# Five projections of a two-layer graph attention kernel: from a 7-product scheme on halves to a 15-product scheme on thirds

## The chip, the cores and the metric

The kernel runs on one core of a Trainium2 chip. The metric is the device time of one execution in microseconds; the time before is the median of three runs, 644.64 us (644.09 to 644.74). All data is fp32 apart from masks. The engines named below are TensorE (PE: matmuls; PEld: its weight loads), VectorE (DVE), ScalarE (ACT), GpSimd (POOL) and SyncE (SP), and the 16 DMA engines that carry out the transfers that SP, POOL and ACT issue.

## The reference

A graph attention network of two layers on 512 nodes with 768 features, a residual and a layer norm. Layer 1 has 8 heads, layer 2 has one.

```python
def gat_layer(x, W, a_s, a_d, b, edge_index, concat):
    n = x.shape[0]
    H, C = a_s.shape
    h = (x @ W).reshape(n, H, C)
    src, dst = (edge_index[0], edge_index[1])
    alpha_s = jnp.einsum('nhc,hc->nh', h, a_s)
    alpha_d = jnp.einsum('nhc,hc->nh', h, a_d)
    e = jax.nn.leaky_relu(alpha_s[src] + alpha_d[dst], NEG_SLOPE)
    m = jax.ops.segment_max(e, dst, num_segments=n)
    e = jnp.exp(e - m[dst])
    denom = jax.ops.segment_sum(e, dst, num_segments=n)
    alpha = e / (denom[dst] + EPS)
    msg = h[src] * alpha[:, :, None]
    out = jax.ops.segment_sum(msg, dst, num_segments=n)
    out = out.reshape(n, H * C) if concat else out.mean(axis=1)
    return out + b

h = gat_layer(x, W1, a_src1, a_dst1, b1, edge_list, concat=True)   # W1 768 x 6144
h = jax.nn.elu(h)
out = gat_layer(h, W2, a_src2, a_dst2, b2, edge_list, concat=True) # W2 6144 x 768
x = _layernorm(x + out, axis=-1)
```

The projection is `x @ W`: for one head 512 x 768 by 768 x 768.

## The kernel before

The edges are counted once into a dense 512 x 512 matrix (`cnt`), so that attention is a masked softmax times this count, and the sums over edges are matmuls. The heads of layer 1 then go through a loop (L874 to L977), and each pass of it has three stretches of work on TensorE:

- `mixed` (L783): the attention matrix of head h+1 times its features, 21 products of 256 columns, which gives the transposed output of the head; `elu` (L736) writes it to `gT`.
- `second` (L358): `gT` of that head times its 768 rows of W2, added into `h2`.
- `projection` (L333): x times the columns of W1 of head h+2, into `hs`.

Each of the three uses a scheme of seven products for blocks of 2 x 2 (halves of 256 nodes and of 384 features). For the projection there are 7 products x 2 row tiles of 128 nodes x 3 parts of the sum (`product`, L311), 42 matmuls of 128 x 128 by 128 x 384. The operands on the left, `XA`, are blocks of the transposed x (`xT`) and three sums of such blocks (`xS`); they are made once (`left`, L290), one of them in place in `xT`. The operands on the right are blocks of the weights and four sums: `t1` and `t3` are made while loading, by a plain transfer from SP and an accumulating one from POOL onto it (L107/L108, L119); `t2` and `t4` by VectorE (L307, L308).

The order on each engine's queue is written out by hand: an instruction stands in its engine's queue where the program calls it (`manual_schedule`). What matters around the change:

- Weights have two slots. `load_w1(h + 2)` goes into slot "w2" at the top of a pass (L876). `load_w2(h + 1)` goes into slot "w1" at the end of `second` (L949), behind the four transposing transfers of the attention matrix (`turn_out`, L730). For each, SP issues `t1` and six blocks of 128 rows, POOL the two additions (0.59 MB each).
- `attended` (L859) loads operands into `w2t2` and `w2t4`; VectorE reads them (`attend`) right after the projection's first product has been issued.
- In the projection's loop (L954 to L974) VectorE empties the banks of PSUM (ten of fourteen, L350 to L354; ScalarE the others), makes the sums for the next `mixed` (`left_sums`, `right_sums`), the sums of the weights of the coming `second` (`sums2`), and the logits of two node tiles. The pool `mm` has five banks.
- `row_out` (L474) sends a row of logits through DRAM by SP, to be broadcast; `lift` (L486) of the next `second` reads it.

## Time and profile before

| What | us |
|---|---|
| median of three runs | 644.64 |
| the profiled execution | 644.97 |
| its span, first to last instruction | 643.2 |
| granted clock of TensorE, mean share | 0.999 |
| one pass of the loop (227.05 to 299.61) | 72.56 |
| in it: `mixed`, `second` and projection | 18.38, 54.18 together |
| VectorE busy in that `mixed`, `second`, projection | 14.72, 21.98, 20.66 |

The page gives per group of instructions the source line, the engine, the operation, the output and inputs by the program's names, the shape, the count, the busy time and the mean ns of one instruction. The line is that of the helper, so all products of `projection` and `second` stand under L315, and are told apart by their tiles: `xT` and `xS` are the projection's, `gT` and `gS` those of `second`. An fp32 matmul is two instructions. In a timeline each line has the start, the length, the engine, the source line, the operation and its tiles; SPq and POOLq are the queues that issue transfers. In a table of stretches each line has the stretch, its length, the busy time and the instructions of PE, PEld, DVE, ACT and POOL, the granted clock, the busy share of the DMA engines and what they moved in GB/s.

### The profile page before, as it was taken

To read this page: it belongs to the slowest core of one execution; us is meant where nothing else is said; L and a number is where in the kernel's file an instruction comes from. 1 tells how busy PE (TensorE), PEld (TensorE's weight loads), DVE (VectorE), ACT (ScalarE), POOL (GpSimd) and SP (SyncE) were. 2 spreads that over 40 slices of the span, in tenths; PEclk is the share of its full clock that TensorE was granted. 3 is DMA by queue.
4 is the path that set the end of the run, shared out by engine and by line. 5 is a ranking of instruction groups with operands and counts; after the bars stand their busy time and mean duration, and the time that the engine had idled before them with its cause. 6 is when DMAs were issued, how large, how long until landed. Compare 5 with 4: busy or idle time off the path is not lost.

```text
span 643.2 us, 7161 instructions
## 1 busy us (share of the span) xinstructions
PE 633.0 (98%) x2329; PEld 403.0 (63%) x2329; DVE 515.8 (80%) x1124; ACT 281.9 (44%) x476; POOL 46.2 (7%) x90
## 2 busy tenths in 40 slices
PE   8999999999999999999999999999999999999995
PEld 5555586557755586556755586556855586645553
DVE  8979889978789777877789677877789677876775
ACT  5874745530726045530726045430726035543440
POOL 1300011011000010011000110011000110000000
PEclk9999999999999999999999999999999999999999
DMA  8993488796706794196716794196806890410222
GB/s 295 326 235 88 84 239 276 161 267 202 190 21 170 157 254 139 35 267 193 197 29 162 165 256 139 33 264 202 191 30 155 219 258 16 107 50 0 32 59 77
DMA packets 81096, 100.32 MB, mean 156 GB/s; under 512 B 39654, under 2 KB 63006, under 8 KB 81054
## 3 DMA queue, kind: packets, MB, share of 16 engines
q1 hardware_dynamic: 67646, 78.57, 39.5%
q0 software_dynamic: 12976, 20.65, 18.5%
q10 hardware_dynamic: 432, 0.59, 0.3%
q8 instruction: 20, 0.33, 0.2%
q14 instruction: 22, 0.18, 0.1%
HBM read 86.93 MB, written 1.59 MB: 138 GB/s over the span
## 4 chain that ended last, share of the span: by engine, by line
PE 97%; ACT 1%; DVE 1%; issue 0%; DVEq 0%; ACTq 0%
PE mm L315 65%; PE mm L805 20%; PE mm L751 3%; PE mm L1086 3%; PE held L315 2%; PE tr L580 1%; PE bc L184 1%; PE held L460 1%; PE bc L580 0%; ACT os L552 0%; PE mm L213 0%; PE tr L1010 0%; DVE os L554 0%; PE tr L719 0%; ACT xT L214 0%
## 5 line engine op out<-in xcount | busy, mean ns | idle before, releaser
L315 PE MATMUL mm<-w,gT 128*128 128x384 f32 x288 | 96.3, 487 | 0.0
L315 PE MATMUL mm<-w,xT 128*128 128x384 f32 x264 | 88.2, 487 | 0.0
L315 PEld LDWEIGHTS mm<-w,gT 128*128 128x128 f32 x288 | 54.5, 190 | 37.2 <-issue 1.6
L315 PEld LDWEIGHTS mm<-w,xT 128*128 128x128 f32 x264 | 49.9, 190 | 35.3 <-ACT os L552 0.8
L809 ACT COPY u<-mm 128x256 f32<-128x256 f32 x21 | 7.8, 373 | 140.5 <-PE mm L805 140.5
L499 ACT ACTIVATE q<-q,nmax 128x512 f32<-128x512 f32 x36 | 25.8, 721 | 88.3 <-DVE nmax L497 88.3
L805 PE MATMUL mm<-PT,hs 128*128 128x256 f32 x252 | 61.3, 379 | 0.0
L315 PE MATMUL mm<-w1t,gS 128*128 128x384 f32 x180 | 60.6, 487 | 0.0
L315 PE MATMUL mm<-w2t,xS 128*128 128x384 f32 x168 | 56.6, 487 | 0.0
L805 PEld LDWEIGHTS mm<-PT,hs 128*128 128x128 f32 x252 | 47.8, 190 | 8.4 <-issue 0.4
L315 PEld LDWEIGHTS mm<-w1t,gS 128*128 128x128 f32 x180 | 34.1, 190 | 24.0 <-DVE w1t L307 0.5
L375 DVE TENSOR_TENSOR h<-h,mm 128x384 f32<-128x384 f32 x72 | 39.1, 550 | 12.5 <-PE mm L315 12.0
L315 PEld LDWEIGHTS mm<-w2t,xS 128*128 128x128 f32 x168 | 31.8, 190 | 22.4 <-ACT q L488 0.4
L805 PE MATMUL mm<-pS,gS 128*128 128x256 f32 x168 | 43.2, 380 | 0.0
L733 ACT COPY PT<-zr 128x1024 uint16<-128x1024 uint16 x34 | 39.5, 1161 | 2.6 <-DMA zr<-pS 2.0
L805 PEld LDWEIGHTS mm<-pS,gS 128*128 128x128 f32 x168 | 31.8, 190 | 4.7 <-DVE pS L778 0.4
L728 ACT COPY pS<-q 128x1024 uint16<-128x1024 uint16 x26 | 27.2, 1044 | 16.7 <-DVE q L713 16.7
L315 PE MATMUL mm<-w,gS 128*128 128x384 f32 x96 | 32.6, 486 | 0.0
L315 PE MATMUL mm<-w,xS 128*128 128x384 f32 x96 | 32.5, 487 | 0.0
L315 PE MATMUL mm<-w1t,gT 128*128 128x384 f32 x96 | 32.3, 486 | 0.0
L375 DVE TENSOR_TENSOR u<-u,mm 128x384 f32<-128x384 f32 x28 | 15.4, 553 | 18.8 <-PE mm L315 18.7
L108 POOL DMA_DIRECT2D w1t<-in_L_gnn_W_dram x7 | 8.9, 1267 | 299.0 <-DVE hs L768 171.7
(192 smaller groups left out, 1080.6 us busy)
## 6 DMA issues: line engine op xcount, KB each, us to landing
w<-in_L_gnn_W_dram SPq DMA_DIRECT2D x91, 384.0 KB
w<-in_L_gnn_W_dram POOLq DMA_DIRECT2D x16, 576.0 KB, 8.6
w2t<-in_L_gnn_W_dram SPq DMA_DIRECT2D x10, 576.0 KB
w1t<-in_L_gnn_W_dram SPq DMA_DIRECT2D x9, 576.0 KB
w2t<-in_L_gnn_W_dram POOLq DMA_DIRECT2D x8, 576.0 KB, 8.9
w1t<-in_L_gnn_W_dram POOLq DMA_DIRECT2D x7, 576.0 KB, 8.5
a_s<-in_L_gnn_a_src_dram SPq DMA_DIRECT2D x8, 384.0 KB
a_d<-in_L_gnn_a_dst_dram SPq DMA_DIRECT2D x8, 384.0 KB
```

Source lines behind the costliest of these rows:

```text
L108: nc.gpsimd.dma_start(t1, upper[:, :, R], accum_op=ALU.add)
L184: nc.tensor.matmul(idle, zeros[:, :P], zeros, start=True, stop=True)
L315: nc.tensor.matmul(ps[:, :HALF], A_[p][:, k, i * P:(i + 1) * P], B_[p][:, k, :], start=start and k == 0, stop=k == HK - 1, skip_group_chec ...
L375: nc.vector.tensor_tensor(a, a, ps, op=ALU.subtract if p == "P7" else ALU.add)
L460: nc.tensor.matmul(bank["P1", i][:, :HALF], XA["P1"][:, k, i * P:(i + 1) * P], B_["P1"][:, k, :], start=k == 0, stop=k == HK - 1, skip_gro ...
L499: nc.scalar.activation(q, q, AF.Exp, bias=nmax, scale=-1.0)
L728: nc.scalar.copy(apart.rearrange("p (h n) -> p h n", h=2), q.bitcast(U16).rearrange("p (n h) -> p h n", h=2))
L733: nc.scalar.copy(PT.rearrange("p s n -> p (s n)").bitcast(U16).rearrange("p (s n h) -> p s n h", s=NT, h=2)[:, :, t * P:(t + 1) * P, :], p ...
L751: nc.tensor.matmul(ps[:, :N], HS[h][:, s, c * P:(c + 1) * P], PT[:, s, :], start=(s == 0), stop=(s == NT - 1))
L805: nc.tensor.matmul(bank[p][:, :HN], A_[p][:, k, c * P:(c + 1) * P], B_[p][:, k, :], start=over is None and k == 0, stop=k == 1, skip_group ...
L809: nc.scalar.copy(u, part("P1"))
L1086: nc.tensor.matmul(ps[:, :cols.stop - cols.start], PT[:, s, t * P:(t + 1) * P], h2[:, s, cols], start=(s == 2), stop=(s == 1))
```

## The change

For heads 3 to 7 the projection uses another scheme. x is cut into 2 halves of nodes and 3 thirds of features, the head's weights into 3 x 3 thirds, and 15 products take the place of the 18 of a plain block product. A product is 2 row tiles x 2 parts of the sum, 4 matmuls of 128 x 128 by 128 x 256, so there are 60 of them. The two row tiles lie beside each other in one bank, and each product is emptied by one instruction of 128 x 512. Five chains of products share five banks; within a chain a product is added to what lies in the bank, after the emptying of the one before.

Fifteen left operands come from x. Three are blocks of `xT` as they are (`P2`, `P4`, `P0`), three are sums put in place of blocks of it (`P8`, `P9`, `P13`), and four sums (`P11`, `P10`, `P12`, `P5`) lie in `xS`. Five (`P7`, `P1`, `P6`, `P3`, `P14`) are made in `gT`, which is overwritten in each pass, so they are stored once to DRAM (`xd`, 128 x 2560) and loaded again ahead of each projection (`reload_x`, behind the transposes and ahead of `load_w2`). They are made in the pass of head 2, whose projection keeps the old scheme, and the last ones in the next `mixed` and `second`.

The weights: `load_thirds` issues six row blocks and two plain blocks of 0.26 MB on SP, and four additions of 0.26 MB on POOL; `rest` issues P11's plain block and its addition after the projection has begun, and VectorE makes eight sums of 512 columns in the projection's loop. The slot "w2" is now one tile of six row blocks, not two of three. Of the two sums of W2 one is made in the projection's last step, the other in the next `mixed`.

The diff, with the parts that only unpack tiles left out:

```diff
+    xdram = ctx.enter_context(tc.tile_pool(name="xdram", bufs=1, space=bass.MemoryType.DRAM))
...
-        W[h] = []
-        for r in range(2):
-            w = wpool.tile([P, HK, D], F32, name=f"{slot}{r}")
-            for k in range(r * HK, (r + 1) * HK):
-                nc.sync.dma_start(w[:, k - r * HK, :], m[k * P:(k + 1) * P, :])
-            W[h].append(w)
-        W[h].append(t1)
+        if slot == "w2":
+            rows_ = wpool.tile([P, DC, D], F32, name="w2r")
+            W[h] = [rows_[:, :HK], rows_[:, HK:], t1]
+        else:
+            W[h] = [wpool.tile([P, HK, D], F32, name=f"{slot}{r}") for r in range(2)] + [t1]
+        for k in range(DC):
+            nc.sync.dma_start(W[h][k // HK][:, k % HK, :], m[k * P:(k + 1) * P, :])
...
+    def load_thirds(h):
...
+        rows_, pair_ = wpool.tile([P, DC, D], F32, name="w2r"), flat(1)
+        add = ALU.add
+        for k in range(DC):
+            nc.sync.dma_start(rows_[:, k, :], m[k * P:(k + 1) * P, :])
+            if k == 3:
+                nc.gpsimd.dma_start(third(rows_, 1, 1), part(1, 2), accum_op=add)
+            if k == 5:
+                nc.gpsimd.dma_start(third(rows_, 2, 1), part(0, 1), accum_op=add)
+        for j, (k0, k1, n) in enumerate(((0, 2, 2), (0, 1, 0))):
+            nc.sync.dma_start(square(pair_, j), part(k0, n))
+            nc.gpsimd.dma_start(square(pair_, j), part(k1, n), accum_op=add)
+        raw = {(k, n): third(rows_, k, n) for k in range(3) for n in range(3)}
+        B_ = dict(P8=raw[0, 2], P9=raw[0, 0], P5=raw[0, 1], P13=square(pair_, 0), P12=square(pair_, 1),
+                  P14=raw[2, 1], P4=raw[2, 0], P0=raw[1, 2], P3=raw[2, 2], P7=raw[1, 0], P1=raw[1, 1])
+        def rest():
+            two, four = flat(2), flat(4)
+            B_.update(P6=square(two, 0), P2=square(two, 1), P11=square(four, 0), P10=square(four, 1))
+            nc.sync.dma_start(B_["P11"], part(0, 1))
+            nc.gpsimd.dma_start(B_["P11"], part(1, 1), accum_op=add)
...
+            return dict(P6=op("P6", "P14", "P4", ALU.subtract), P4=op("P4", "P13", "P4", add),
+                        P2=op("P2", "P12", "P13", ALU.subtract), P10=op("P10", "P5", "P1", add),
+                        P0=op("P0", "P12", "P0", add), P1=op("P1", "P6", "P1", add),
+                        P3=op("P3", "P10", "P3", ALU.subtract), P7=op("P7", "P6", "P7", add))
+        return B_, rest
...
+    def by_thirds(h, A_, B_):
...
+                first = chain not in bank
+                if first:
+                    bank[chain] = mm.tile([P, 512], F32, name="mm")
+                for i in range(2):
+                    for k in range(2):
+                        nc.tensor.matmul(bank[chain][:, i * TH:(i + 1) * TH], A_[p][:, k, i * P:(i + 1) * P], B_[p][:, k, :],
+                                         start=first and i == k == 0, stop=k == 1, skip_group_check=True)
+            def empty():
+                ps = bank[chain].rearrange("p (i n) -> p i n", i=2)
+                if how in (1.0, -1.0):
+                    nc.scalar.activation(out(o), ps, AF.Copy, scale=how)
+                else:
+                    nc.vector.tensor_tensor(out(o), out(o), ps, op=how)
...
+            ("P8", "a", (1, 2), 1.0), ("P13", "x", (1, 2), minus), ("P9", "b", (1, 0), 1.0), ("P2", "y", (0, 0), 1.0),
+            ("P4", "x", (1, 0), plus), ("P12", "y", (1, 0), minus), ("P6", "x", (1, 1), 1.0), ("P0", "y", (1, 2), plus),
+            ("P1", "z", (0, 1), -1.0), ("P10", "y", (1, 1), minus), ("P5", "z", (1, 1), plus),
+            ("P14", "x", (0, 1), minus), ("P11", "y", (0, 1), plus), ("P7", "x", (0, 0), minus),
+            ("P3", "y", (0, 2), -1.0))]
...
+    def x_thirds():
...
+        again_ = op(xT[:, :HK, HN:], xT[:, :HK, :HN], xT[:, :HK, HN:], minus)
+        store = lambda: nc.sync.dma_start(stored, gF[:, :RELOAD * 2 * TH])
...
+    def reload_x():
+        nc.sync.dma_start(gF[:, :RELOAD * 2 * TH], stored)
...
         if 0 < h < H - 2:
-            load_w1(h + 2)()
+            B3, rest_of_thirds = load_thirds(h + 2)
...
-        finish = mixed(h, AA, BB, besides + [d_ for _, d_ in halves])
-        besides = []
+        finish = mixed(h, AA, BB, besides + [d_ for _, d_ in halves] + behind)
+        besides, behind = [], []
...
                 turn_out(q[3], 3)
+                if 0 < h:
+                    reload_x()
                 load_w2(h + 1)()
             e1()
-        if h + 2 < H:
+            for f in in_second[:1]:
+                f()
+            del in_second[:1]
+        if 0 < h and h + 2 < H:
+            for f in attend:
+                f()
+            sums = rest_of_thirds()
+            pairs = by_thirds(h + 2, XB, B3)
+            AA, sums3 = left_sums(h + 1)
+            B2, sums2 = right(W2[h + 1], "w1")
+            for n in range(15):
+                pairs[n][0]()
+                for p in {0: ("P6", "P2"), 1: ("P4",), 4: ("P10",), 5: ("P0",), 6: ("P1",), 9: ("P7",),
+                          12: ("P3",)}.get(n, ()):
+                    sums[p]()
+                if n == 5:
+                    BB, rsums_ = right_sums()
+                    sums3 += rsums_
+                if n in (2, 3, 5, 6, 8, 9, 10):
+                    for _ in range(2 if n == 8 else 1):
+                        sums3.pop(0)()
+                if n in (11, 13):
+                    logits(h + 2, HS[h + 2], 2 + (n - 11) // 2)
+                if n == 14:
+                    sums2[0]()
+                    behind = sums2[1:]
+                pairs[n][1]()
+                if n in (1, 2, 4):
+                    turn_in((n + 2) // 2)
+            assert not sums3
+        elif h + 2 < H:
...
-                if n in (9, 10):
+                if n == 0:
+                    XB, early, again_, store, late_ = x_thirds()
+                if n in (2, 4, 6, 8, 9):
+                    early.pop(0)()
+                if n == 9:
+                    store()
+                if n == 9:
+                    again_()
+                if n == 12:
+                    late_.pop(0)()
                     sums2.pop(0)()
+                    behind = sums2 + late_[:2]
+                    in_second = late_[2:]
```

More of the change, by code (lines that the diff above doesn't have):

```diff
@@ L121, in load_w, with third, square, part @@
         return rest
+    TH = 2 * P
+    def third(rows_, k, n):
+        return rows_[:, 2 * k:2 * k + 2, n * TH:(n + 1) * TH]
+    def square(t_, j):
+        return t_[:, j * 2 * TH:(j + 1) * 2 * TH].rearrange("p (k n) -> p k n", k=2)
+    def load_thirds(h):
+        m = w1[:, h * D:(h + 1) * D]
+        def part(k, n):
+            return m[k * TH:(k + 1) * TH, n * TH:(n + 1) * TH].rearrange("(k p) d -> p k d", p=P)
+        def flat(j):
+            return wpool.tile([P, HK, HALF], F32, name=f"w2t{j}").rearrange("p k n -> p (k n)")
+        rows_, pair_ = wpool.tile([P, DC, D], F32, name="w2r"), flat(1)
[17 more added lines that the diff above has]
+            nc.gpsimd.dma_start(B_["P11"], part(1, 1), accum_op=add)
+            def op(o, a, b, how):
+                return lambda: nc.vector.tensor_tensor(B_[o], B_[a], B_[b], op=how)
+            return dict(P6=op("P6", "P14", "P4", ALU.subtract), P4=op("P4", "P13", "P4", add),
[3 more added lines that the diff above has]
+        return B_, rest
     def load_w1(h, slot="w2"):
@@ L356, in projection, with out, step, multiply @@
         return [pair(p, i, start, empty) for p, start, empty in steps for i in range(2)]
+    def by_thirds(h, A_, B_):
+        HS[h] = hs = hpool.tile([P, NT, D], F32, name="hs")
+        new_alpha(h)
+        bank = {}
+        def out(o):
+            return hs[:, 2 * o[0]:2 * o[0] + 2, o[1] * TH:(o[1] + 1) * TH]
+        def step(p, chain, o, how):
+            def multiply():
+                first = chain not in bank
[11 more added lines that the diff above has]
+                    nc.vector.tensor_tensor(out(o), out(o), ps, op=how)
+            return multiply, empty
+        plus, minus = ALU.add, ALU.subtract
+        return [step(*a) for a in (
+            ("P8", "a", (1, 2), 1.0), ("P13", "x", (1, 2), minus), ("P9", "b", (1, 0), 1.0), ("P2", "y", (0, 0), 1.0),
[3 more added lines that the diff above has]
+            ("P3", "y", (0, 2), -1.0))]
     def second(h, A_, B_):
@@ L832, in gat_pass, with op, negative @@
     load_a(1, a_src1[1], a_dst1[1])
+    gF, xF = gT.rearrange("p c n -> p (c n)"), xS.rearrange("p a k n -> p (a k n)")
+    RELOAD = 5
+    stored = xdram.tile([P, RELOAD * 2 * TH], F32, name="xd")
+    def x_thirds():
+        a = {(i, k): xT[:, 2 * k:2 * k + 2, i * TH:(i + 1) * TH] for i in range(2) for k in range(3)}
+        X = dict(P2=a[0, 0], P4=a[1, 2], P0=a[1, 1], P8=a[0, 2], P13=a[0, 1], P9=a[1, 0])
+        X.update({p: square(gF, j) for j, p in enumerate(("P7", "P1", "P6", "P3", "P14"))})
+        X.update({p: square(xF, j) for j, p in enumerate(("P11", "P10", "P12", "P5"))})
+        def op(o, u, v, how):
+            return lambda: nc.vector.tensor_tensor(o, u, v, op=how)
+        def negative(o, u, v):
+            return lambda: nc.vector.scalar_tensor_tensor(o, u, -1.0, v, op0=ALU.mult, op1=ALU.subtract)
+        plus, minus = ALU.add, ALU.subtract
+        early = [op(X["P7"], a[0, 0], a[0, 1], minus), op(X["P1"], X["P7"], a[0, 2], minus),
+                 op(X["P6"], a[1, 2], X["P1"], minus), op(X["P3"], a[0, 2], a[0, 0], minus),
+                 negative(X["P14"], a[0, 2], a[1, 2])]
+        again_ = op(xT[:, :HK, HN:], xT[:, :HK, :HN], xT[:, :HK, HN:], minus)
+        store = lambda: nc.sync.dma_start(stored, gF[:, :RELOAD * 2 * TH])
+        late_ = [op(X["P10"], X["P1"], a[1, 1], minus), op(X["P11"], a[0, 1], a[1, 1], plus),
+                 negative(X["P12"], a[0, 0], a[1, 1]), op(X["P8"], a[1, 0], a[1, 2], minus),
+                 op(X["P5"], X["P10"], X["P8"], plus), op(X["P9"], a[1, 0], a[1, 1], minus),
+                 negative(X["P13"], a[0, 0], a[1, 2])]
+        return X, early, again_, store, late_
+    def reload_x():
+        nc.sync.dma_start(gF[:, :RELOAD * 2 * TH], stored)
     AA, lsums = left_sums(0)
@@ L872, in attended @@
                 times(R, b1_[:, D:], -1.0, V2)]
+    behind, in_second = [], []
     for h in range(H - 1):
         if 0 < h < H - 2:
-            load_w1(h + 2)()
+            B3, rest_of_thirds = load_thirds(h + 2)
         elif h:
```

## The prediction

> **What bounds the kernel now.** I read the busy times first, then the chain of waits, then one head's period at the level of the queues.

> ```profile
> PE 633.0 (98%) x2329; PEld 403.0 (63%) x2329; DVE 515.8 (80%) x1124; ACT 281.9 (44%) x476; POOL 46.2 (7%) x90
> PE 97%; ACT 1%; DVE 1%; issue 0%; DVEq 0%; ACTq 0%
> ```

> TensorE is busy nearly all the time, and the chain that ended last runs on it. From the chain in order of time (start, length):

> ```profile
> 227.05 18.38 PE mm L805 x84
> 245.43 54.18 PE mm L315 x168
> 299.61 18.38 PE mm L805 x84
> ```

> A head takes 72.56 us with no gap: 42 mixed products (L805), then 84 of L315, which are `second` and the projection, 27.09 us each. An fp32 matmul is two instructions here, so 42 matmuls of 384 columns are 84 instructions of 54.18 / 168 = 322.5 ns. This projection starts at 272.36 (its first `w,xT` matmul); I call that T0. For 256 columns the page says this of one instruction, and the timeline of TensorE this of the step from group to group:

> ```profile
> L805 PE MATMUL mm<-pS,gS 128*128 128x256 f32 x168 | 43.2, 380 | 0.0
> 305.49 1.03 PE L805 MATMUL mm<-PT,hs 128*128 128x256 f32 x4
> 306.36 1.03 PE L805 MATMUL mm<-pS,gS 128*128 128x256 f32 x4
> ```

> The 380 ns include overlap. Four instructions start every 0.862 us (six such steps from 305.49 to 310.67), so the price is 215.5 ns, 0.842 ns a column, against 0.840 at 384 columns: narrow products cost nothing extra.

> The change also puts transfers into the projection. The queues of SP and POOL around T0:

> ```profile
> 266.12 7.08 SPq L730 DMA_TRANSPOSE zr<-pS  x3
> 273.89 1.23 SPq L730 DMA_TRANSPOSE zr<-nr  x1
> 275.23 0.52 SPq L107 DMA_DIRECT2D w1t<-in_L_gnn_W_dram  x1
> 275.84 3.37 SPq L113 DMA_DIRECT2D w<-in_L_gnn_W_dram  x6
> 280.47 1.26 POOL L108 DMA_DIRECT2D w1t<-in_L_gnn_W_dram  x1 [47.59 <-PE mm L315]
> 283.41 1.27 POOL L119 DMA_DIRECT2D w<-in_L_gnn_W_dram  x1 [1.67 <-DMA w<-in_L_gnn_W_dram]
> ```

> and the stretches of that time (last columns: granted clock, DMA share, GB/s):

> ```profile
> 278.00:282.00 4.00, 4.00 (x14) 2.31 (x13) 2.60 (x3) 3.09 (x4) 1.26 (x1) 1.00 1.04 407
> 282.00:284.00 2.00, 2.00 (x8) 1.17 (x7) 1.42 (x2) 0.00 (x0) 0.59 (x1) 1.00 1.02 376
> 284.00:286.00 2.00, 2.00 (x8) 1.21 (x7) 1.16 (x2) 0.00 (x0) 0.68 (x1) 1.00 1.04 214
> 286.00:288.00 2.00, 2.00 (x8) 1.21 (x7) 1.16 (x2) 0.00 (x0) 0.00 (x0) 1.00 1.17 205
> 288.00:291.00 3.00, 3.00 (x11) 1.74 (x10) 2.18 (x4) 0.00 (x0) 0.00 (x0) 1.00 1.15 201
> 291.00:293.00 2.00, 2.00 (x8) 1.14 (x6) 1.22 (x3) 0.00 (x0) 0.00 (x0) 1.00 0.07 12
> ```

> SP's plain loads of W2 (0.59 + 2.36 MB) run at about 407 GB/s until about 285. Then POOL's two accumulating transfers (0.59 MB each) run at about 203 GB/s until 291.2. In between the DMA engines are full; only after 291 are they free. A transfer added in this stretch moves everything behind it.

> **TensorE's part.** 15 products of 2 x 2 matmuls are 60, or 120 instructions of 215.5 ns: 25.86 us, 1.724 a product. That is 1.23 less than 27.09; over five heads 6.15 us. If nothing is late, this is the gain.

> **The transfer that is late: P11.** Its block is loaded in `rest_of_thirds`, after the projection has begun, since its slot (`w2t4`) is used by `attend` until 2.9 us after T0. In SP's program order it stands behind `reload_x` and all of `load_w2`, and it then needs a POOL addition, which stands behind the two of `load_w2`. Step by step, on this head's clock:
> 1. `reload_x` takes the place of the L107 issue at 275.23. It is 128 x 2560 x 4 B = 1.31 MB; at 407 GB/s 3.2 us. The plain loads of W2 end at 288.2 instead of 285.
> 2. P11's plain block, 0.26 MB: 0.65 us, to 288.9.
> 3. POOL sees it some 2 us later: t1 and the first three rows of W2, 1.77 MB, have moved by about 281.4, and the L119 addition that waits for them is issued at 283.41. So the issue is at 290.9.
> 4. The additions of W2 share the engines with all this and end 3.85 us later than before, at 295.05. P11's 0.26 MB follow at 203 GB/s: 1.3, to 296.3. From the last byte to the landing take 0.8 (L119: 283.41 + 8.6 median = 292.0, last byte 291.2). P11 is there at 297.1, T0 + 24.8.
> 5. P11 is the thirteenth product, due at T0 + 12 x 1.724 = 20.7. It is 4.1 us late, and P7 and P3 are queued behind it on TensorE.

> The projection then lasts 24.8 + 3 x 1.724 = 29.95 us, 2.86 more than 27.09. Heads 3 to 7: **+14.3 us**.

> No row has a 0.26 MB addition. The nearest landings are:

> ```profile
> w<-in_L_gnn_W_dram POOLq DMA_DIRECT2D x16, 576.0 KB, 8.6
> w2t<-w2t POOLq DMA_DIRECT2D x2, 576.0 KB, 5.7
> ```

> From 290.9 they give 296.6 and 299.5: 3.5 to 6.4 us late, +2.3 to +5.2 a head, 656 to 671. If the reload cost nothing, everything is 3.2 earlier, P11 is 0.9 late and a head gains 0.3. I take 4.1, since the order of the additions gives it by their own rate, and nothing in the stretch shows room for 1.31 MB more.

> [...]

> **VectorE.** The projection's window:

> ```profile
> 272.40:299.60 27.20, 20.66 (x33) 1.00 0.78 199
> ```

> Out go ten emptyings of 384 columns (0.55), the two sums L307/L308 of `w2t` (1.35 each) and one of `w1t`. In come nine emptyings of 512 (0.42 at 256 and 0.55 at 384 make 0.68) and eight sums of 512 (0.685, as L777): 20.66 - 5.5 - 4.05 + 6.1 + 5.5 = 22.7 of 25.86 us. It fits, with one tight place: P14's emptying stands behind the logits of tile 2 (2.0 us), which start at about T0 + 19.65. It ends at 22.3; P7, on the same bank, is due at 22.4. Without P11's delay a stall here could cost up to 0.6 a head. With it the cost is nothing. After P11 only 2.0 + 0.7 + 1.35 us are left in the queue beside 3.45 us of products, and the next mixed block asks VectorE for nothing in its first 1.7 us. The W2 sum that moves into that block (1.35, its window 14.7 of 18.4) ends up in the 1.51 us of idle that VectorE has at 247.40 before the first L375. Without that cover, 1.35 a head.

> **ScalarE.** Eight copies of 0.48 become six of 0.59 (L720's size): nothing; it is busy 6.2 of 27 us.

> **Other moves, costed at nothing.** The reloaded operands are first needed by P6, T0 + 10.3. They are moved by about 280 and there by 282 at the latest, T0 + 9.6; a delay here would only use up part of P11's. `load_thirds` now waits for the whole old tile, so its rows start at the projection's end, not 3.4 us before; with four additions (1.05 MB) it is done some 17 us later, and its first use is 45 us away. The row broadcast of `row_out` queues behind it; `lift` needs it 20 us after the projection and `leak` comes another 5 later. If those were used up, the softmax would be late, about 3 us a head. The moved sums of W2 need its first addition, landed by 293 and asked for at T0 + 26.

> **The second head, once.** `x_thirds` adds 5 + 1 sums of 0.685 and one of 0.95 to VectorE's projection window and takes 1.35 away (24.4 of 27.1), then 2 x 0.685 + 1.35 to the next mixed block (17.4 of 18.4) and 5 x 0.685 to the next `second` (22.0 to 25.4 of 27). Bounds 0 and 3 us; as the windows stay below full, I take 0.5. The store falls where the DMA engines now move 12 GB/s.

> **Sum.** The profiled execution took 644.97 (span 643.2, 1.77 around it), 0.33 above the median 644.64. 644.97 + 14.3 + 0.5 = 659.8; as a median, **659.5**.

> **Rivals.**
> - *P11 in time (0.16).* The 16 DMA engines take P11's block earlier or add it faster. Then the columns' gain stands: 644.6 - 6.15 + 1 for the tight place and the second head = 639.5, up to 643. The deciding point is a delay of 1.23 us, an arrival at T0 + 21.9. For it: only 3 us separate that from my sum, and the reload's price is inferred. An addition that doesn't queue behind the other two takes its issue (1.27), its bytes (1.3) and the 0.8 to the landing: from 290.9 to 294.3, just that point; with a reload that overlaps the transposes too, it is below it. [...] Against it: the stretch from 278 to 291 is full.
> - *VectorE is the bound (0.05).* P11 in time, but the 2 us of logits hold banks: 0.6 to 1.3 a head, 642 to 645. For: 88% busy. Against: one tight place in fifteen.
> - *The clock falls in the wait (0.11).* TensorE has no long gap in the trace but its end:

> ```profile
> 636.00:638.00 2.00, 0.40 (x4) 0.20 (x2) 1.50 (x7) 0.29 (x1) 0.00 (x0) 1.00 0.04 11
> 641.00:642.00 1.00, 0.00 (x0) 0.00 (x0) 0.00 (x0) 0.00 (x0) 0.00 (x0) 0.79 0.00 0
> ```

>   There the granted clock falls some 5 us after the last matmul, longer than a wait of 4.1. If it falls within such a wait, up to 5.2 us of products run at half clock: 2.6 a head, 659.5 + 13 = 672 at most, 666 if every second wait is hit. [...]

> **Chances.** 0.68 for the forecast, its own range 652 (the reload at half its price) to 671 (the upper landing); 0.11, 0.16 and 0.05 for the rivals. A measurement here tells 0.2% from no change, 1.3 us. Slower: 0.68 + 0.11 - 0.02 = 0.77; same 0.03; faster 0.20. To leave out no more than 2 in 10 the range has to reach to the fast case: 639 to 668, with the top of the first and third case left out.

> **What would show it.** Right: on TensorE a gap of about 4 us ahead of the product that reads `w2t` at P11's place, released by a POOL transfer, in five projections; the additions in the DMA table reaching 3.9 us further; 120 instructions at 215.5 ns. Wrong: P11's addition landing before T0 + 21; gaps released by VectorE or at P6; a clock below 1.00 in the projections.

## The result, and the profile after

The changed kernel takes 675.34 us (median of four runs, 673.94 to 677.39) against 644.37 before: 1.0483 times as long, 95% interval 1.0455 to 1.0511. The forecast was 659.5, and its range ended at 668. The profiled execution took 677.39 us, its span 675.6.

From the page, the busy times and the engines of the chain that ended last:

```profile
PE 641.9 (95%) x2509; PEld 445.3 (66%) x2509; DVE 537.9 (80%) x1162; ACT 289.9 (43%) x486; POOL 63.6 (9%) x105
PE 86%; DMA 8%; DVE 2%; issue 1%; ACT 1%; SPq 0%; DVEq 0%; POOLq 0%; ACTq 0%
```

TensorE is busy for 642 us instead of 633, although it has fewer columns to do, and transfers are now a part of the chain. A pass of the loop takes 78.5 to 78.8 us instead of 72.56; `mixed` (18.38) and `second` (27.10) are as before, so the whole of it is in the projections. One of them in the timeline of TensorE (T0, the projection's start in the chain, is 280.65 here):

```profile
299.48 1.89 PE L423 MATMUL mm<-w2r,gT 128*128 128x256 f32 x8
305.80 3.75 PE L423 MATMUL mm<-w2t,xS 128*128 128x256 f32 x8 [4.43 <-DMA w2t<-in_L_gnn_W_dram]
309.35 4.48 PE L423 MATMUL mm<-w2r,gT 128*128 128x256 f32 x16
```

Twelve products run as forecast, 1.73 us each. Then P11 waits 4.43 us for a transfer, and the three last products take 8.03 us (305.80 to 313.83) instead of 5.2. The queues of SP and POOL in that projection:

```profile
283.36 0.52 SPq L948 DMA_DIRECT2D gT<-xd  x1
284.45 3.02 SPq L116 DMA_DIRECT2D w<-in_L_gnn_W_dram  x6
289.45 0.38 SPq L161 DMA_DIRECT2D w2t<-in_L_gnn_W_dram  x1
294.47 1.26 POOL L120 DMA_DIRECT2D w<-in_L_gnn_W_dram  x1 [1.67 <-DMA w<-in_L_gnn_W_dram]
301.25 1.22 POOL L162 DMA_DIRECT2D w2t<-in_L_gnn_W_dram  x1 [5.51 <-DVE hs L431]
```

L948 is the reload, L116 the rows of W2, L161 and L162 are P11's two transfers. The bracket of the last row names an emptying by VectorE, which that addition does not read. In the chain that ended last, the step before the addition is P11's plain block, which is on its way for 10.96 us (start, length):

```profile
289.45 10.96 DMA w2t<-in_L_gnn_W_dram
301.25 4.42 DMA w2t<-in_L_gnn_W_dram
```

And the stretches around the wait (length; busy time of PE, PEld, DVE, ACT, POOL; granted clock, DMA share, GB/s):

```profile
288.00:292.00 4.00, 4.00 (x20) 3.51 (x20) 2.94 (x5) 1.24 (x2) 0.48 (x1) 1.00 1.01 395
296.00:300.00 4.00, 4.00 (x20) 3.51 (x20) 3.27 (x6) 0.60 (x1) 0.00 (x0) 1.00 1.10 204
302.00:304.00 2.00, 0.00 (x0) 0.00 (x0) 1.63 (x4) 0.00 (x0) 0.46 (x1) 1.00 0.96 155
304.00:306.00 2.00, 0.20 (x1) 0.23 (x2) 0.00 (x0) 0.00 (x0) 0.00 (x0) 0.56 0.53 80
306.00:308.00 2.00, 2.00 (x5) 1.62 (x6) 0.00 (x0) 0.00 (x0) 0.00 (x0) 0.50 0.03 8
312.00:314.00 2.00, 2.00 (x11) 1.77 (x10) 2.00 (x4) 0.14 (x1) 0.00 (x0) 1.00 0.00 0
```

The additions run until about 305 (P11's lands at 305.67), and in the wait the granted clock falls to half: the stretch from 306 holds 5 matmul instructions, the one from 312 holds 11. All five projections look like this: waits of 4.66, 4.43, 4.21, 4.88 and 4.91 us, each with a fall of the clock.

### The profile page after: what moved, and what is told of

Read it like the earlier page. It is cut to its first block, busy times and chain, and to the rows that moved or that the text cites. A ratio compares the mean times of both kernels' runs of the same rounds, so it can differ in the third digit from the quotient of the medians.

```text
span 675.6 us, 7677 instructions
## 1 busy us (share of the span) xinstructions
PE 641.9 (95%) x2509; PEld 445.3 (66%) x2509; DVE 537.9 (80%) x1162; ACT 289.9 (43%) x486; POOL 63.6 (9%) x105
## 4 chain that ended last, share of the span: by engine, by line
PE 86%; DMA 8%; DVE 2%; issue 1%; ACT 1%; SPq 0%; DVEq 0%; POOLq 0%; ACTq 0%
PE mm L364 41%; PE mm L889 18%; PE mm L423 14%; DMA w2t<-in_L_gnn_W_dram 7%; PE mm L835 3%; PE mm L1246 3%; PE held L364 2%; DMA gT<-xd 2%; PE tr L664 1%; PE held L544 1%; PE bc L233 1%; PE bc L664 0%; DVE scr L379 0%; ACT os L636 0%; PE mm L262 0%
## 5 line engine op out<-in xcount | busy, mean ns | idle before, releaser
L364 PE MATMUL mm<-w,gT 128*128 128x384 f32 x252 | 83.6, 486 | 0.0
L429 ACT ACTIVATE hs<-mm 128x512 f32<-128x512 f32 x30 | 17.9, 597 | 128.3 <-PE mm L423 110.3
L364 PEld LDWEIGHTS mm<-w,gT 128*128 128x128 f32 x252 | 47.9, 190 | 31.9
L431 DVE TENSOR_TENSOR hs<-hs,mm 128x512 f32<-128x512 f32 x45 | 30.8, 685 | 43.4 <-PE mm L423 43.3
L423 PE MATMUL mm<-w2t,xS 128*128 128x256 f32 x120 | 37.7, 469 | 23.1 <-DMA w2t<-in_L_gnn_W_dram 23.1
L423 PEld LDWEIGHTS mm<-w2t,xS 128*128 128x128 f32 x120 | 27.8, 236 | 29.7 <-issue 24.9
L889 PE MATMUL mm<-pS,gS 128*128 128x256 f32 x168 | 43.2, 380 | 0.0
L423 PE MATMUL mm<-w2r,gT 128*128 128x256 f32 x160 | 40.8, 407 | 0.0
L423 PE MATMUL mm<-w2r,xT 128*128 128x256 f32 x160 | 37.8, 379 | 0.0
L423 PEld LDWEIGHTS mm<-w2r,gT 128*128 128x128 f32 x160 | 33.8, 211 | 5.9
L423 PEld LDWEIGHTS mm<-w2r,xT 128*128 128x128 f32 x160 | 30.4, 190 | 5.2
## 6 DMA issues: line engine op xcount, KB each, us to landing
w1t<-in_L_gnn_W_dram SPq DMA_DIRECT2D x9, 576.0 KB
w<-in_L_gnn_W_dram POOLq DMA_DIRECT2D x8, 576.0 KB, 9.5
w1t<-in_L_gnn_W_dram POOLq DMA_DIRECT2D x7, 576.0 KB, 9.6
```

Of the source, the lines that this page charges most:

```text
L364: nc.tensor.matmul(ps[:, :HALF], A_[p][:, k, i * P:(i + 1) * P], B_[p][:, k, :], start=start and k == 0, stop=k == HK - 1, skip_group_chec ...
L423: nc.tensor.matmul(bank[chain][:, i * TH:(i + 1) * TH], A_[p][:, k, i * P:(i + 1) * P], B_[p][:, k, :], start=first and i == k == 0, stop= ...
L429: nc.scalar.activation(out(o), ps, AF.Copy, scale=how)
L431: nc.vector.tensor_tensor(out(o), out(o), ps, op=how)
L889: nc.tensor.matmul(bank[p][:, :HN], A_[p][:, k, c * P:(c + 1) * P], B_[p][:, k, :], start=over is None and k == 0, stop=k == 1, skip_group ...
```

## The experiments

The theory after the result: P11's transfers land late (4.6 us a head), and the wait drops the clock (2.5 us a head more); the scheme's columns are worth what they promise. Rivals: the scheme itself is slow, or the slow last products have another cause.

**P11's transfers ahead of the W2 load.** For the heads concerned `load_w2` is called after `rest_of_thirds` instead of ahead of it.

```diff
                 if 0 < h:
                     reload_x()
-                load_w2(h + 1)()
+                else:
+                    load_w2(h + 1)()
...
             sums = rest_of_thirds()
+            load_w2(h + 1)()
```

> P11's two transfers are issued ahead of the W2 load instead of behind it; nothing else changes. Theory (P11 lands late, and the wait drops the clock): P11's plain block now stands right behind the reload on SP and its addition is POOL's first, so it lands about T0 + 14, ahead of T0 + 20.7; no gap at P11, clock 1.00 throughout, each of the five projections 25.9 to 26.5 us instead of 33.2, the kernel 641 to 644 us. Rival (the scheme itself is slow: VectorE's fuller queue or narrow products): the projections stay above 29 us and the kernel above 655.

Measured: 641.40 us (640.75 to 641.58), ratio 0.9952, interval 0.9939 to 0.9966. From its queues and from its chain in order of time:

```profile
275.71 0.38 SPq L161 DMA_DIRECT2D w2t<-in_L_gnn_W_dram  x1
282.87 1.20 POOL L162 DMA_DIRECT2D w2t<-in_L_gnn_W_dram  x1 [42.32 <-DMA w1t<-in_L_gnn_W_dram]
```

```profile
272.38 26.15 PE mm L423 x120
```

P11's addition is issued 10.5 us into the projection instead of 20.6, and no wait is left at P11: its product starts at 292.93, 10.1 us after that issue, right behind the one before it. The mean granted clock of the execution is 0.998 (0.973 in the changed kernel, 0.999 before). The projections take 26.15 to 26.24 us, but the first of the five 26.89, with 0.47 us of waiting at P2's product. One call moved is worth 34 us. The rival falls: VectorE's fuller queue and the narrow products are as before, and four of the five projections come within 0.4 us of the 25.86 that the products alone need. The plain load and the addition were moved together; which of the two counts for more was not tried.

**TensorE kept busy in the wait.** Transfers as in the changed kernel, with matmuls into a spare bank ahead of P11.

```diff
+                if p == "P11":
+                    spare = bc.tile([P, 512], F32, name="bc")
+                    for _ in range(18):
+                        nc.tensor.matmul(spare[:, :P], ident, ident, start=True, stop=True)
```

> 18 matmuls of the identity with itself (128 columns, about 0.215 us each, 3.9 us) stand ahead of P11's product, so TensorE is busy while it waits; P11 lands when it did. Theory: the clock stays at 1.00, the three products after the wait take 5.2 us instead of about 8, five times 2.9 us come back: 677.4 - 14.3 = 663 us. Rival (the slow products after the wait have another cause than the idle time, or the clock falls for the transfers' sake): 674 to 678 us with a clock of 0.5 after the wait.

Measured: 664.90 us (one run), with waits of 0.4 to 1.7 us left in four of the five projections (3.3 us together). Of the 2.9 us a head that the forecast counted for the clock 2.5 came back (677.39 to 664.90 in the profiled executions). The stretches of one wait, and the three products behind it in the chain:

```profile
300.00:302.00 2.00, 2.00 (x19) 1.91 (x18) 0.34 (x1) 0.00 (x0) 0.00 (x0) 1.00 0.93 136
302.00:304.00 2.00, 1.27 (x7) 1.07 (x7) 0.00 (x0) 0.00 (x0) 0.00 (x0) 1.00 0.01 2
```

```profile
302.83 5.42 PE mm L427 x24
```

P11's addition lands as late as in the changed kernel (25.5 us after the projection's first matmul, 25.2 there), but the clock stays at 1.00 in these stretches, and the last three products take 5.42 us in all five passes. So the fall of the clock comes from the idle time. It cost some 12.5 of the 32.4 us between the two profiled executions (644.97 and 677.39): these three products in five passes took 39.6 us in the changed kernel, and would take 27.1 at this rate.

**A shorter filling.** The same with `range(8)`.

> Only 8 of the identity matmuls (1.7 us) ahead of P11's product, so each of the five waits still leaves TensorE idle for 2.5 to 3.2 us. [...] Rival (the clock falls a fixed time after the last matmul, the 3.0 us of the pass at 304 or the 5 us of the kernel's end): none of the waits of under 3.0 us brings a fall, 663 to 666 us with a clock of 1.00.

Measured: 668.67 us (one run). The waits were 2.79, 2.93, 2.58, 2.07 and 3.57 us, and the clock fell in the first, third and fifth; each fall cost 1.7 us (the last three products took 7.11 instead of 5.42). The time lies above the 663 to 666 of the rival. The falls begin at 227.05, 380.65 and 534.25, 153.60 us apart both times, and in the 3.41 us behind each the granted clock is 0.50. 153.60 is 45 times 3.413, so stretches of 3.41 us were laid off from the first fall. Some of them, with TensorE's busy time (the columns after the count are granted clock, DMA share, GB/s):

```profile
223.64:227.05 3.41, 1.14 (x5) 1.00 0.48 75
227.05:230.46 3.41, 3.41 (x9) 0.50 0.02 5
298.72:302.13 3.41, 2.27 (x19) 1.00 1.03 171
302.13:305.54 3.41, 1.63 (x8) 1.00 0.26 40
377.24:380.65 3.41, 0.83 (x5) 1.00 0.56 84
```

The wait of 2.93 us (300.98 to 303.91) is cut in two by the border at 302.13 and leaves 2.27 and 1.63 us of work in its stretches: no fall. The wait of 2.58 (377.31 to 379.89) lies within one and leaves 0.83: a fall. A delay after the last matmul, the rival, would have dropped the longer of the two first.

**Without the reload.** `reload_x()` is not called.

> The reload of the five sums of x is left out, so the products that use them get other numbers; all else as in the changed kernel. Theory (the reload's 1.31 MB pushes everything behind it): P11 lands 3.2 us earlier, its wait shrinks from 4.4 to about 1.2 us, too short for the clock to fall, and the kernel comes to 677.4 - 5 x (3.2 + 2.9) = 647 us. Rival (the reload runs in DMA time that was free, P11 waits for the queue of POOL additions only): wait still above 4 us, 675 or more.

Measured: 652.08 us (one run); this missed the 647 by 5. The first wait at P11 in TensorE's timeline:

```profile
224.37 3.35 PE L423 MATMUL mm<-w2t,xS 128*128 128x256 f32 x8 [2.47 <-DMA w2t<-in_L_gnn_W_dram]
```

The five waits are 2.47, 1.46, 1.16, 1.68 and 1.82 us, so the reload is what makes most of the delay (2.9 us of it a head, the mean going from 4.62 to 1.72), close to the 3.2 of the forecast. But they are half a microsecond longer than expected, and behind the first, of 2.47 us, the last three products took 7.11 us, where they took 5.42 behind the four others: the same 1.7 us that a fall cost in the run with 8 matmuls. The reload could delay P11 by its bytes, or because SP stands at P11's plain load until the reload has landed (up to 1.9 us a head); the run does not separate the two. That the DMA engines were full meanwhile (share 1.01, 395 GB/s from 288 to 292 in the changed kernel) speaks for the bytes. Even without the reload P11 would be late behind W2.

**VectorE's tight place.** On top of P11 first: of tile 2's two logits one stands behind P14's emptying, and P3's sum is made at product 7 instead of 12.

```diff
-                for p in {0: ("P6", "P2"), 1: ("P4",), 4: ("P10",), 5: ("P0",), 6: ("P1",), 9: ("P7",),
-                          12: ("P3",)}.get(n, ()):
+                for p in {0: ("P6", "P2"), 1: ("P4",), 4: ("P10",), 5: ("P0",), 6: ("P1",), 7: ("P3",),
+                          9: ("P7",)}.get(n, ()):
...
-                if n in (11, 13):
-                    logits(h + 2, HS[h + 2], 2 + (n - 11) // 2)
+                if n in (11, 12):
+                    half_logits(h + 2, 2)[n - 11]()
+                if n == 13:
+                    logits(h + 2, HS[h + 2], 3)
```

> On top of the run with P11 first: of tile 2's two logits one now stands behind P14's emptying, and P3's sum is made five products earlier. Theory (the 0.2 to 0.3 us by which those projections exceed 25.9 us are P7's wait for P14's emptying, the one tight place): projections 25.9 us, five times 0.25 us less, 640.2 us. Rival (they come from another wait): 641.4 us, no change.

Measured: 639.85 us (639.63 to 640.85), ratio 0.9935, interval 0.9919 to 0.9950. P14's emptying in VectorE's timeline, first with P11 first alone, then with this edit:

```profile
294.07 0.68 DVE L431 TENSOR_TENSOR hs<-hs,mm 128x512 f32<-128x512 f32 x1
```

```profile
292.76 0.69 DVE L431 TENSOR_TENSOR hs<-hs,mm 128x512 f32<-128x512 f32 x1
```

It starts 21.7 us after the projection's start (272.38) in the first, and 20.8 after it (272.00) in the second. In the first, P7, on the same bank, starts at 294.81, when this emptying has just ended (294.75); in the second it follows P11 without a pause. The projections come to 25.90 to 25.99 us, except for the first of the five (26.63, with P2's wait). The ranges of the two runs touch, but the projections differ by 0.25 us in four of five passes, as expected. It is the split of the logits that moves the emptying: P3's sum stood behind it already. So the tight place that the forecast named is real and cost 0.25 us a head, as long as nothing hid it.

**The second head's pass.** On top of P11 first: there the first sum of W2 is made two products earlier, and the sums of x in the next `second` come two at a time. In the first form P10's sum was moved into the next `mixed` too, where it reads a block that has been overwritten, so heads 3 to 7 get another operand.

> On top of the run with P11 first, in the second head's pass alone: the first sum of W2 is made two products earlier, one sum of x moves from the projection's end to the next mixed block, and the sums in the next second stretch are made two at a time in its first half. Theory (VectorE's queue runs 3 us past that projection's end and 1.4 us past that second's end, which costs 0.8 us in the mixed block and 0.6 at P2's product): 1.0 to 1.5 us less, 640.2 us. Rival (the mixed block is slow for its own longer queue): at most 0.5 us less.

Measured: 640.44 us (640.33 to 641.02), 1.0 less than with P11 first by the medians, but the two ranges overlap. In the profiled executions the stretch from the end of the `mixed` block before to the end of the first new projection is only 0.5 us shorter (126.80 us instead of 127.32): `mixed` (18.52) and the projection (26.28) gain 1.3, but `second` takes 27.70 us instead of 27.10. This run alone does not decide between theory and rival. Together with the split logits:

> The edits of the two runs above together. Theory (separate places, gains add): 638.9 to 639.3 us, 0.8% under the kernel before. Rival (they share one queue's slack): no better than the better of the two.

Measured: 639.12 us (639.08 to 640.00), ratio 0.9922, interval 0.9908 to 0.9935; 2.3 less than with P11 first, where the two edits alone gave 1.6 and 1.0. Then with P10's sum left in the projection:

```diff
+                if n == 10:
+                    sums2.pop(0)()
                 if n == 12:
                     late_.pop(0)()
-                    sums2.pop(0)()
...
-            for f in in_second[:1]:
+            for f in in_second[:2]:
```

> As the run with both edits, but P10's sum stays in the second head's projection, ahead of the overwriting of the block that it reads; only the W2 sum is made earlier there, and the sums of the next second stretch stand two at a time. Theory (what is gained lies at P2's product and in the mixed block's late start): VectorE's queue runs 1.3 us less past the projection's end, the mixed block takes 18.4 to 18.8 us, P2's wait of 0.47 us is gone, 639.1 to 639.5 us. Rival (P10's sum in the mixed block was what helped): 639.9 us as with the logits split alone.

Measured: 638.83 us (638.38 to 639.45), a little below the forecast, ratio 0.9915, interval 0.9901 to 0.9928. Its chain from the second head's `mixed` on:

```profile
153.64 18.52 PE mm L889 x84
172.16 27.26 PE mm L364 x84
199.42 25.90 PE mm L423 x120
```

With P11 first alone these were 19.2, 27.10 and 26.9 us; the mixed block keeps 0.14 of its 0.8, and P2's wait is gone. The rival for P10's sum falls: the time lies below every run with the split logits alone (639.63 to 640.85). This kernel is the fastest of the study, 0.85% under the kernel before.

## Why the prediction was right about the delay and wrong about the time

- **The columns' gain: right.** Forecast 1.23 us a head; 27.09 became 25.90 where nothing waits, 1.19.
- **P11's delay: right, slightly small.** Forecast there at T0 + 24.8 and 4.1 us late; measured T0 + 25.0 in the pass shown (landed at 305.67) and 4.2 to 4.9 late, together 23.1 us instead of 20.5. (Counted from the timeline's first matmul, as the prediction counts, the measured times are 0.16 more.) Inside the working two errors cancel: POOL could issue the addition only at T0 + 20.6, not 18.5, since P11's plain block, given 0.65 us and some 2 us until POOL sees it, was on its way for 10.96 us; but the landing came 4.4 us after the issue, not 6.2. That the arrival fits to some 0.3 us is in part luck.
- **The reload's price: right in size.** 3.2 forecast, 2.9 measured in the run without it; that it is the bytes, as the prediction has it, is not shown apart from SP's stand behind the reload.
- **The step that failed: leaving the clock out of the sum.** The prediction took the 5 us between the last matmul and the fall at the kernel's end for a delay, called it "longer than a wait of 4.1", and gave the fall 0.11 as a rival, at up to 2.6 us a head and 672 us. All five waits brought it, some 2.5 to 3.4 us after they began, at 2.5 us a head, 12.5 in all; with waits also longer than 4.1 the time passed even the 672. The end's row shows no fixed delay: in the kernel before, that fall comes 5.2 us after the last matmul (636.39 to 641.58, 0.50 from there on), at the end of the changed kernel 4.0 us after it (668.90 to 672.90). The run with 18 matmuls gives most of the loss back (675.3 to 664.9); in that with 8 a wait of 2.58 us brought a fall and one of 2.93 did not, and the falls go with the work in the 3.41 us ahead of them (0.25 to 1.14 us), not with the length of the wait alone.
- **The second head: too small.** 0.5 forecast; 0.8 us in its mixed block and some 0.7 in the projection with P2's wait (26.89 against 26.15) were measured.
- **Costed at nothing: right for most.** The reload is there before P6 needs it, the moved W2 sums and the later start of the weights' loads show no wait. The tight place at P14 cost nothing beside P11's delay and 0.25 us a head once that was gone, less than the 0.6 given for it. VectorE was busy for 23.5 us of a projection without waits, where 22.7 were forecast. The line on ScalarE misread its row: the eight instructions of that window hold four copies, not eight, so the change adds copies there; no wait on ScalarE in the projections came of it.

Of the 17.6 us between the forecast for a profiled execution (659.8) and 677.39, the clock is 12.5, the longer waits 2.6, the second head 1.0, the columns 0.2; some 1.3 us, short pauses of issue among them, are not assigned.

## What to carry to other kernels

A small transfer that an engine needs soon belongs ahead of a large one that is needed late: order both the plain loads on SP and the accumulating ones on POOL by due time, not by where the program is most easily written (675.34 against 641.40 us here). Where a sum says that TensorE will wait for microseconds, put the clock into the price at once: here waits of 2.47 and 2.58 us cost 1.7 us each behind them and those of 4.2 to 4.9 about 2.5, while waits of 2.07 and 2.93 cost nothing more. Until the wait itself can be removed, matmuls that serve only to fill it can keep the clock: 18 did so in all five waits, 8 in two. In this kernel the scheme with fewer products was worth its columns only after the queues around it had been put in order again: 0.85% gained, where the first form lost 4.8%.
